# Two cross-attention layers: in the first layer, even entries hold their image tokens before their text tokens, and one product group makes the image values of both mixed tiles

## The chip, the cores and the metric

The kernel runs on one core of a Trainium2 chip. A core has a matrix engine (TensorE, PE in the profile; its weight loads are listed apart as PEld), a vector engine (VectorE, DVE), a scalar engine (ScalarE, ACT), GpSimd (POOL) and SyncE (SP), which here only issues transfers. Products land in PSUM banks; all else lies in SBUF, 128 partitions wide, or in DRAM. Transfers are carried by the core's sixteen DMA engines. The metric is the device time of one execution in microseconds, as the median of several runs.

## What is computed

Two attention layers follow each other, over B = 16 entries of S = 256 query rows with C = 320 channels and H = 20 heads of D = 16. Both read the same context of 256 tokens of width 512 for each entry. The change concerns the first layer alone:

```python
TEXT_LEN, SEM_SCALE = 77, 0.5
text = encoder_hidden_states[:, :TEXT_LEN]      # 77 tokens
ip = encoder_hidden_states[:, TEXT_LEN:]        # 179 tokens
q = hidden_states @ Wq
k_text, v_text = text @ Wk, text @ Wv
...
text_out = softmax(q_h @ k_text_h * scale) @ v_text_h          # by heads
...
text_probs = softmax(q @ k_text * scale)                       # all channels at once
sem = (text_probs @ text) @ ip * scale
fused = q_h @ ip_k_h * scale + SEM_SCALE * sem[:, None]        # ip_k = ip @ Wk_ip
ip_probs = softmax(fused) * spatial_mask
out = (text_out + ip_probs @ ip_v_h) @ Wout + bout + residual  # ip_v = ip @ Wv_ip
```

So every query attends to 77 text tokens and to 179 image tokens, with a softmax of its own for each kind and other weights for keys and values of each kind. The second layer is alike, with 252 text and 4 image tokens; it is not touched.

## The kernel before

**Slots.** The first layer is worked off in 80 slots: 16 entries times five groups of four heads, slot k being group k % 5 of entry k // 5. In the middle of the first layer ten slots, that is two entries or one pair, take some 75 us. Into the gaps between the attention steps of a slot the function `fill` puts steps of tasks that prepare later entries: each task has a list of times, in slots, at which its steps are due. TensorE's instructions stand in the order in which this text issues them; a scheduler orders the other engines, within the dependencies.

**The context of a pair.** Entries are prepared two at a time. `context` loads the transposed context of a pair, four blocks of 128 of the 512 input rows by 2 x 256 tokens, into tiles `ct` (tags `cta`, `ctb`), and splits it into a rounded high part and the rest, as every product is made of three (high times high, high times low, low times high). In such a tile the first entry's text comes first, then its image, then the second entry's text and image.

**Values.** `values0_` (L412) makes the values of an entry as three tiles of 128 tokens by 320 columns: tile 0 is tokens 0 to 127 with the text weights (`wv0`), tile 1 the same tokens with the image weights (`wvi0`), tile 2 tokens 128 to 255 with the image weights. Tokens 0 to 127 are mixed, 77 text and 51 image, so this mixed tile is made twice, once for each kind, and ACT's copy out of PSUM multiplies by a mask of rows that keeps text rows in the one and image rows in the other. Each tile is a group of twelve products (four blocks, three terms). The 17th column of every head in these tiles holds a mark, the mask itself, which gives the sums of the softmax; it is written once at the start (`marks`).

**Keys and stacks.** `keys0` makes the keys of a pair, text with `wk0` and image with `wki0`, and sends them to DRAM. For each slot `stacks0` (L697), called four slots ahead (`LEAD`), builds two stacks in SBUF, for four heads side by side: in the key stack (`ks`, four buffers in turn) rows 0 to 47 are the keys, rows 48 to 124 the matrix M of the entry (half the products of its 77 text tokens with its image tokens; zero for text columns), rows 125 and 126 two indicator rows, -1 for text and for image tokens. In the query stack (`qs`) stand the queries, the text probabilities (`tph`, 77 rows), and the maxima of the scores. M is made by `tokens0` (L424). A slot needs M and `tph` anew for the first four of an entry's five groups; the fifth finds them in its buffer. The text columns of rows 48 to 124 are set to zero once, at the start, and M's transfer writes the image columns alone (L710); the indicator rows too are written once for each of the four buffers (`fields`, L343). All of SP's transfers are issued by the helper `dma`, so L83 is their line in the profile, and their tiles tell them apart: M's are `ks<-M`.

**A slot's attention.** `score0` (L730) multiplies rows 0 to 124 of both stacks for two slots ahead, and DVE takes the maxima over text (L738) and image columns (L739). `maxima0` (L741) turns them with a small product (L745), ACT copies them out (L747) and sends them into the query stack's last two rows (L749, `qs<-mt`). `turned0` (L751) multiplies all 127 rows into turned scores (L761), from which the indicator rows take the maxima; ACT makes exponentials (L764) and POOL multiplies them by a correction (L767). `attend0` multiplies them with the value tiles (L794), and `settle0` divides (L805 and on).

The order of a slot k on TensorE is: maxima of slot k + 1, first half of the scores of slot k + 2, first half of the turned products of slot k, prepared steps, attention of slot k - 1, second half of the scores, second half of the turned products, then the stacks of slot k + 4 are asked for, and prepared steps again.

Of the kernel before, what the change touches and what calls it, by code (L numbers as in the profile page):

```python
# [17 lines left out]
S = 256  # L18
H = 20
# [7 lines left out]
T1 = S - NIP  # L27
DUP = S // 2 - NIP
# [21 lines left out]
def xattn2(  # L50
# [60 lines left out]
    words, slots = {"ctb": 1024, "cta": 1024, "raw": 512, "rawc": 512, "both": 2 * (S - T0), "kb": 936, "si": 256, "sp": 128, "wC": 2 * 4 * (H * D + NIP), "mt": S, "mx": 2, "tmp": (NG + 1) * 48, "kst": 4 * S, "rs": 2 * S, "P": 4 * S}, {}  # L111
# [77 lines left out]
    def in_turn(parts, wait, tag="raw", eng=nc.vector, later=False):  # L189

        ahead, parts, tags = [], list(parts), tag.split()
        for i in range(len(parts) + 1):
            if len(tags) > 1:
                new = () if i else range(len(parts))
            else:
                new = range(i + 1 if i else 0, min(i + 2, len(parts)))
            if i:
                halves(*ahead.pop(0), eng, wait)
            for j in new:
                src, hi, lo = parts[j]  # L200
                raw = buf(tags[j // 2 % len(tags)], [128, 512], bufs=2)
                shape = src.shape
                raw = raw[:, : shape[1]] if len(shape) == 2 else raw.rearrange("p (k n) -> p k n", k=shape[1])
                (queued if later else lambda inst: inst)(dma(raw, src))
                ahead.append((hi, lo, raw))
            if wait:
                yield
# [53 lines left out]

    def context(b, n, wait=0):

        tiles, parts = [], []
        for k in range(0, 4, 3 - n):
            src = cT_d[:, b * S : (b + n) * S].rearrange("(k p) t -> p k t", p=128)[:, k : k + 3 - n]
            ct = buf("cta" if n == 1 or k < 2 else "ctb", [128, 2, 512], FR, bufs=SIZES["CTA" if n == 1 or k < 2 else "CTB"], name="ct")
            split = lambda t: t.rearrange("p (k t) -> p k t", t=n * S)
            parts.append((src, split(ct[:, 0]), split(ct[:, 1])))
            tiles.append(ct)  # L270
        yield from in_turn(parts, wait, "rawc raw" if b == 2 and n == 2 else "rawc", nc.gpsimd if wait and b != 2 else nc.vector, n == 2 and b > 2)
        if n == 2:
            return lambda s, k: tiles[k][:, s].rearrange("p (b t) -> p b t", b=2)
# [12 lines left out]
    ct = [buf(t, [128, 2, 512], FR, bufs=2, name="ct") for t in ("cta", "cta", "ctb", "ctb")]  # L286
    ct0 = {0: lambda s, k, tiles=ct: tiles[k][:, s].rearrange("p (b t) -> p b t", b=2)}
# [27 lines left out]
    hsn = const_tile([128, 3, 8, 2, 16], "hsn")  # L315

    def constants():
# [3 lines left out]
        for i in range(SIZES["NR"]):  # L321
            nc.gpsimd.memset(f(ks[i]), 0.0)
# [10 lines left out]

    def fields():
# [7 lines left out]
        for i in range(SIZES["NR"]):  # L342
            dma(ks[i][XROW + T0 : KS0], ind0r.unsqueeze(1).to_broadcast([2, 4, S]))  # L343
# [16 lines left out]
    def keys0(c):  # L360
# [8 lines left out]
        for m in range(3):  # L369
            kst = buf("kst", [128, 2, 2, S], FR, bufs=SIZES["KST"])  # L370
            for w, lo, hi, a, z in ((wk0, 0, T0 + 1, 0, T0), (wki0, T0 - 1, S, T0, S)):
                kp = bank()[:, : 2 * (hi - lo)].rearrange("p (b t) -> p b t", b=2)
                prod_m(kp, w, m, lambda s, k: ct(s, k)[:, :, lo:hi], 4)
                n = 64 if m == 2 else 128
                evacuate(kst[:, 0, :, a:z], kst[:, 1, :, a:z], kp[:, :, a - lo : z - lo], m)
                if a:
                    keys_out(kd[0][c], m, kst)
                else:
                    nc.gpsimd.tensor_copy(kt[:n, m, :, :, :T0], f(kst[:n, :, :, :T0]))
                yield  # L380

    def keys_first():

        ct = ct0[0]
# [27 lines left out]
    def values0_(b):  # L412
        ct, i = ct0[b // 2], b % 2
        V = vr[(b + 2) % 3]
        for t, (w,), lo, sc in ((0, wv0, 0, tmask[:, 0:1]), (1, wvi0, 0, tmask[:, 1:2]), (2, wvi0, 128, 1.0)):
            vp = bank()[:, :320]
            prod(vp, lambda s, k: ct(s, k)[:, i, lo : lo + 128], lambda s, k: w(s, k), 4)
            nc.scalar.activation(
                vcols(V, V0W)[:, t, :, 0:16], vp.rearrange("p (h d) -> p h d", d=D), AF.Copy, scale=sc
# [4 lines left out]
    def tokens0(b):  # L424

        ct, i = ct0[b // 2], b % 2
        M = buf("M", [T0, 2, S], FR, bufs=SIZES["M"])
        nc.gpsimd.memset(f(M[:, :, :T0]), 0.0)
        gp = bank()
        lo = 64  # L430
        prod(gp[:T0, : S - lo], lambda s, k: ct(s, k)[:, i, :T0], lambda s, k: ct(s, k)[:, i, lo:S], 4)
        src = gp[:T0, T0 - lo : S - lo]
        nc.scalar.activation(M[:, 0, T0:], src, AF.Copy, scale=0.5)
        nc.vector.scalar_tensor_tensor(M[:, 1, T0:], src, 0.5, f(M[:, 0, T0:]), op0=ALU.mult, op1=ALU.subtract)
# [211 lines left out]
    def semantic0(b):  # L646
# [40 lines left out]
        for t in range(2):  # L687
            mm(rp[:, t], mh[:, 0, t * 128 : (t + 1) * 128], tph[:, 1], start=True, stop=False)
            mm(rp[:, t], mh[:, 1, t * 128 : (t + 1) * 128], tph[:, 0], start=False, stop=True)
# [7 lines left out]
    def stacks0(k, parts="KQTM"):  # L697
        b, g = divmod(k, NG)
        Q, K = QK[k] = qs[k % SIZES["NR"]], ks[k % SIZES["NR"]]
        for part in parts:  # L700
# [4 lines left out]
            elif g < SIZES["NR"]:  # L705
# [3 lines left out]
                else:  # L709
                    dma(K[XROW : XROW + T0, :, T0:], mh[:, 0:1, T0:].to_broadcast([T0, 4, S - T0]))  # L710
# [19 lines left out]
    def score0(k, t):  # L730
# [7 lines left out]
        nc.vector.tensor_reduce(mn[:, t, :, 0], sp[:, :, :T0], axis=AX.X, op=ALU.max)  # L738
        anchor(nc.vector.tensor_reduce(mn[:, t, :, 1], sp[:, :, T0:], axis=AX.X, op=ALU.max))  # L739
# [50 lines left out]
    def values0(k, pv, v, vt):  # L790
        t, o = ((0, 0), (0, S), (1, S))[vt]
        for s in range(4):
# [335 lines left out]
    for c in range(B // 2):  # L1128
# [7 lines left out]
        task(("v0", 2 * c), shifted(n, -7, -5.4, -5), lambda b=2 * c: values0_(b), *k)  # L1136
# [261 lines left out]
```

## Time and profile before

| | us |
|---|---|
| median of three runs | 1509.85 |
| lowest and highest run | 1503.91, 1513.44 |
| profiled execution, its time | 1522.64 |
| profiled execution, its span | 1520.8 |

| engine | busy us of the span |
|---|---|
| PE | 1436.6 |
| POOL | 1215.1 |
| DVE | 1178.0 |
| ACT | 884.4 |

The profile is of one execution. Its span runs from the first to the last instruction; the time beside it has what lies around the span too. Rows of instructions give the line, the engine, the operation, the tiles as out<-in, the shapes as partitions by elements, how many there were, their busy time together in us and the mean of one in ns, then the idle time of the engine just before them and what ended it. Matmuls overlap each other, so the time from one group's start to the next group's start says what a group costs, not the duration of its instructions. Rows of a timeline give start and duration in us. Rows of a stretch give its length, then each engine's busy time with the number of instructions, then the clock that was granted to TensorE as a share of the full one, the mean busy share of the sixteen DMA engines, and what they moved in GB/s. SPq and ACTq are the queues on which SP and ACT issue transfers.

### The profile page before, as it was taken

The page shows a single profiled execution, that of the slowest core. Times are in us where ns is not written, and L with a number is a line of the kernel's source. Part 1 is how long each engine was busy: PE and PEld are TensorE (multiplying, and loading weights), DVE is VectorE, ACT ScalarE, POOL GpSimd, SP SyncE. Part 2 cuts the span into 40 slices and gives each one's busy share as a digit, 9 for nine tenths or more (in the row PEclk, how much of TensorE's full clock was granted, in tenths as well). Part 3 has the DMA queues.
Part 4 walks back from the last instruction along what each step waited for, and adds up shares of the span by engine and source line. Part 5 has one row for each costly group of instructions (what it writes and reads, how often), then busy time and mean ns, then how long its engine had stood idle before and what let it go on. Part 6 is the DMA issues. An engine that isn't in the chain of part 4 may idle for free.

```text
span 1520.8 us, 36025 instructions
## 1 busy us (share of the span) xinstructions
PE 1436.6 (94%) x12726; PEld 1160.9 (76%) x12726; DVE 1178.0 (77%) x2595; ACT 884.4 (58%) x1973; POOL 1215.1 (80%) x1302
## 2 busy tenths in 40 slices
PE   8689999999999989788999999999999999999996
PEld 7678878887888778566777777777777777777764
DVE  5467777777777787867878888888888887788885
ACT  5346555655565555445665666566656666666561
POOL 4359787978888977887688789877988798879785
PEclk9899999999999999899999999999999999999997
DMA  7757766767676766665534444444444344434311
GB/s 237 208 165 216 203 192 197 214 204 209 183 213 210 210 194 172 186 198 156 147 104 120 125 124 118 130 122 114 121 134 124 107 125 131 125 108 113 103 33 37
DMA packets 228815, 233.04 MB, mean 153 GB/s; under 512 B 38410, under 2 KB 198508, under 8 KB 228620
## 3 DMA queue, kind: packets, MB, share of 16 engines
q1 hardware_dynamic: 226428, 229.44, 52.7%
q8 instruction: 102, 1.67, 0.5%
q10 hardware_dynamic: 2208, 1.30, 0.3%
q14 instruction: 77, 0.63, 0.1%
HBM read 118.04 MB, written 77.10 MB: 128 GB/s over the span
## 4 chain that ended last, share of the span: by engine, by line
PE 75%; DVE 7%; DMA 6%; issue 4%; POOL 3%; ACT 3%; SPq 1%; ACTq 0%; DVEq 0%; POOLq 0%
PE X L932 15%; PE X L238 14%; PE P L794 6%; PE X L603 5%; PE P L944 5%; PE S L737 5%; PE P L954 4%; PE T L761 4%; PE T L884 3%; PE S L890 3%; PE X L606 2%; PE X L248 2%; PE X L572 2%; DMA qs<-mt 1%; PE X L1057 1%
## 5 line engine op out<-in xcount | busy, mean ns | idle before, releaser
L767 POOL TENSOR_TENSOR P<-P,rs 128x512 f32<-128x512 f32 x320 | 415.1, 1321 | 102.5 <-ACT P L764 101.5
L923 POOL TENSOR_TENSOR wt<-P,ctb 128x512 f32<-128x512 f32 x320 | 410.3, 1307 | 78.4 <-ACT ctb L922 78.3
L932 PE MATMUL X<-ctb,gm 128*128 128x512 f32 x1120 | 305.6, 402 | 5.9 <-DVE wt L933 5.8
L764 ACT ACTIVATE P<-T 128x512 f32<-128x512 f32 x320 | 175.9, 593 | 158.6 <-PE T L761 100.0
L933 DVE TENSOR_TENSOR wt<-X,wt 128x512 f32<-128x512 f32 x320 | 216.3, 681 | 42.9 <-PE X L932 37.5
L932 PEld LDWEIGHTS X<-ctb,gm 128*128 128x128 f32 x1120 | 195.7, 189 | 39.1 <-DVE wt L933 8.5
L904 ACT ACTIVATE P<-T 128x512 f32<-128x512 f32 x320 | 173.1, 593 | 77.3 <-PE T L884 75.0
L922 ACT ACTIVATE ctb<-P 128x512 fp32r<-128x512 f32 x320 | 186.9, 627 | 38.8 <-PE X L932 35.4
L892 DVE TENSOR_REDUCE mn<-S 128x4 fp32r<-128x1008 f32 x160 | 191.4, 1196 | 0.0
L739 DVE TENSOR_REDUCE mn<-S 128x4 fp32r<-128x716 f32 x160 | 142.4, 890 | 0.0
L794 PE MATMUL P<-P,vr 128*32 128x256 f32 x1920 | 129.5, 402 | 2.2 <-DVE tmp L811 1.9
L737 PE MATMUL S<-ks,qs 125*128 125x256 f32 x640 | 117.5, 307 | 6.0 <-DVE mn L739 1.7
L737 PEld LDWEIGHTS S<-ks,qs 125*128 125x128 f32 x640 | 88.2, 194 | 41.9 <-issue 21.9
L761 PE MATMUL T<-qs,ks 127*128 127x256 f32 x640 | 108.6, 291 | 4.9 <-DMA qs<-mt 3.2
L1020 POOL TENSOR_TENSOR r<-u,rs 128x40 f32<-128x40 f32 (+2 forms) x17 | 108.7, 6395 | 3.6 <-DVE u L1017 3.6
L805 DVE STREAM_TRANSPOSE nt<-P 128x512 f32<-128x512 f32 x80 | 57.0, 713 | 56.8 <-PE P L794 56.3
L761 PEld LDWEIGHTS T<-qs,ks 127*128 127x128 f32 x640 | 91.5, 196 | 7.6 <-ACT P L764 2.1
L738 DVE TENSOR_REDUCE mn<-S 128x4 fp32r<-128x308 f32 x160 | 74.6, 466 | 28.2 <-PE S L737 27.8
L794 PEld LDWEIGHTS P<-P,vr 128*32 128x32 f32 x1920 | 57.7, 114 | 45.6 <-issue 9.5
L944 PE MATMUL P<-P,v1t 128*32 128x256 f32 x1280 | 86.3, 388 | 0.0
L954 PE MATMUL P<-wt,zone 128*32 128x256 f32 x1280 | 84.8, 379 | 0.3 <-DVE wt L933 0.3
L603 PE MATMUL X<-ho,wF 128*128 128x256 f32 x512 | 75.3, 289 | 9.2 <-ACT mt L747 4.7
(279 smaller groups left out, 2987.6 us busy)
## 6 DMA issues: line engine op xcount, KB each, us to landing
qd<-q SPq DMA_DIRECT2D x96, 256.0 KB
qs<-tph SPq DMA_DIRECT2D x64, 308.0 KB
rawc<-in_cT_dram SPq DMA_DIRECT2D x60, 256.0 KB
qs<-qd SPq DMA_DIRECT2D x80, 192.0 KB
ks<-kd SPq DMA_DIRECT2D x80, 192.0 KB
ks<-kd SPq DMA_DIRECT2D x160, 96.0 KB
qs<-qd SPq DMA_DIRECT2D x160, 96.0 KB
kd<-kst SPq DMA_DIRECT2D x57, 256.0 KB
```

What stands on the lines that cost most here:

```text
L238: last = mm(out, lhs(a, k), rhs(b, k), start=i == 0, stop=i == len(terms) - 1)
L737: mm(sp[:, h], Q[: XROW + T0, h, t * 128 : (t + 1) * 128], K[: XROW + T0, h], start=True, stop=True)
L761: mm(st[p][:, j], K[:KS0, 2 * p + j, t * 128 : (t + 1) * 128], Q[:KS0, 2 * p + j], start=True, stop=True)
L764: exp = anchor(nc.scalar.activation(pt, st[p], AF.Exp, scale=SCALE))
L767: anchor(nc.gpsimd.tensor_mul(pt, pt, rs[:, t : t + 1].to_broadcast([128, 2, S])))
L794: mm(pv[32 * s : 32 * s + 32, o : o + S], v[:, vt, h : h + 32], P[k, s // 2][:, t, s % 2], start=vt < 2, stop=vt != 1,)
L892: anchor(nc.vector.tensor_reduce(maxes[k + 2][:, t], sp[:, :, :T1], axis=AX.X, op=ALU.max))
L904: anchor(nc.scalar.activation(P[k, u][:, t], st[u], AF.Exp, scale=SCALE))
L922: nc.scalar.activation(R[k, u][:, t], P[k, u][:, t], AF.Copy, scale=0.5)
L923: anchor(nc.gpsimd.tensor_sub(W[k, u][:, t], P[k, u][:, t], f(R[k, u][:, t])))
L932: mm(yp, gm[:, gb], R[k, u][:, kt], start=i == 0, stop=i == len(blocks[n]) - 1)
L933: nc.vector.tensor_mul(W[k, u][:, n], yp, W[k, u][:, n])
```

## The change

In pairs 1 to 7 (entries 2 to 15) the context tile gets another order: image tokens of the first entry (179), a gap of 26 columns that stays zero or is masked, image tokens of the second entry, text of the first, text of the second, zeros. `pair` names two runs of such a tile at once. Columns 128 to 255 of it then hold the last 51 image tokens of the first entry, the gap, and the first 51 image tokens of the second. For the first entry of the pair (`turned_round`), tokens stand image first: its tile of tokens 0 to 127 is all image, its mixed tile is tokens 128 to 255, with 51 image and 77 text rows. The second entry keeps text first. One group of twelve products with the image weights on columns 128 to 255 gives the image values of both mixed tiles, which ACT copies out twice, with a mask for each. Six groups of value products for a pair become five.

With it go these:

- Each context load of a pair becomes two transfers (image runs and text runs), and the split works on 538 instead of 512 columns.
- The text keys' products are 154 instead of 156 columns wide.
- As the order of tokens now differs between entries, the text columns of M and the indicator rows differ too. The tile M gets two more rows, which hold the indicators, and its transfer writes all 256 columns of 79 rows of the key stack, where it wrote 179 columns of 77 rows. The zeroing of the four key stacks and the four transfers of indicator rows at the start go; two small transfers fill the two M tiles at the start, and two more turn one of them round at entry 2.
- The marks of the value tiles are written by POOL for each entry from 2 on, as the masks differ by entry, two small copies each.
- Times of the value steps move: for even entries from -7, -5.4, -5 to -7, -5.4, -4.4, for odd ones from -4, -3.8, -3.4 to -3.4, -2.4.

In the built programs, TensorE has 84 products 128x320 with the image weights fewer, and SP has 64 transfers `ks<-M` of 79x4x256 where it had 64 of 77x4x179.

```diff
+LI = S - T0
+IB, TA = 205, 384
+TB, TE = TA + T0, TA + 2 * T0
+CW = TB + 128
...
+    def pair(a, start, stride, n):
+
+        (row, rows), (step, _) = a.ap
+        return type(a)(a.tensor, a.offset + start * step, [[row, rows], [stride * step, 2], [step, n]])
+
+    def turned_round(b):
+
+        return b > 1 and b % 2 == 0
+
+    def text_image(b):
+
+        return (slice(LI, S), slice(0, LI)) if turned_round(b) else (slice(0, T0), slice(T0, S))
...
+                row = cT_d[k * 128 : (k + 1) * 128, b * S : (b + 2) * S].rearrange("p (b t) -> p b t", b=2)
+                to = lambda raw: (pair(raw, 0, IB, LI), raw[:, TA:TE].rearrange("p (b t) -> p b t", b=2))
+                src = [(lambda raw: to(raw)[0], row[:, :, T0:]), (lambda raw: to(raw)[1], row[:, :, :T0])]
+                parts.append((src, ct[:, 0, :TE], ct[:, 1, :TE]))
...
-        for i in range(SIZES["NR"]):
-            nc.gpsimd.memset(f(ks[i]), 0.0)
+        for t in slack:
+            nc.gpsimd.memset(f(t), 0.0)
...
-        for i in range(SIZES["NR"]):
-            dma(ks[i][XROW + T0 : KS0], ind0r.unsqueeze(1).to_broadcast([2, 4, S]))
+        for i in range(2):
+            fused.append(buf("M", [T0 + 2, 2, S], FR, bufs=SIZES["M"]))
+            dma(fused[i][T0:, 0], ind0r)
...
     def values0_(b):
         ct, i = ct0[b // 2], b % 2
         V = vr[(b + 2) % 3]
-        for t, (w,), lo, sc in ((0, wv0, 0, tmask[:, 0:1]), (1, wvi0, 0, tmask[:, 1:2]), (2, wvi0, 128, 1.0)):
+
+        def product(w, at, *to):
             vp = bank()[:, :320]
-            prod(vp, lambda s, k: ct(s, k)[:, i, lo : lo + 128], lambda s, k: w(s, k), 4)
-            nc.scalar.activation(
-                vcols(V, V0W)[:, t, :, 0:16], vp.rearrange("p (h d) -> p h d", d=D), AF.Copy, scale=sc
+            prod(vp, lambda s, k: ct(s, k)[:, at : at + 128], lambda s, k: w[0](s, k), 4)
+            for v, t, sc in to:
+                nc.scalar.activation(
+                    vcols(v, V0W)[:, t, :, 0:16], vp.rearrange("p (h d) -> p h d", d=D), AF.Copy, scale=sc
+                )
...
+        if turned_round(b):
+            product(
+                wvi0,
+                128,
+                (V, 1, masks[1]),
+                (vr[(b + 3) % 3], 1, tmask[:, 1:2]),
             )
             yield
         return V
...
-        M = buf("M", [T0, 2, S], FR, bufs=SIZES["M"])
-        nc.gpsimd.memset(f(M[:, :, :T0]), 0.0)
+        text, image = text_image(b)
+        M = buf("M", [T0 + 2, 2, S], FR, bufs=SIZES["M"])
+        if b == 2:
+            for to, at in ((text, slice(0, T0)), (image, slice(T0, S))):
+                dma(M[T0:, 0, to], fused[1][T0:, 0, at])
+        nc.gpsimd.memset(f(M[:T0, :, text]), 0.0)
...
-                    dma(K[XROW : XROW + T0, :, T0:], mh[:, 0:1, T0:].to_broadcast([T0, 4, S - T0]))
+                    dma(K[XROW : XROW + T0 + 2], mh[:, 0:1].to_broadcast([T0 + 2, 4, S]))
...
     def values0(k, pv, v, vt):
         t, o = ((0, 0), (0, S), (1, S))[vt]
+        if turned_round(k // NG):
+            t = 1 - t
```

108 lines of the change are left out of this document (73 added, 35 removed).

## The prediction

> **What bounds the kernel now.** I read the page first: its span, the busy time of the engines and the chain of waits that ended last.
>
> ```profile
> span 1520.8 us, 36025 instructions
> PE 1436.6 (94%) x12726; PEld 1160.9 (76%) x12726; DVE 1178.0 (77%) x2595; ACT 884.4 (58%) x1973; POOL 1215.1 (80%) x1302
> PE 75%; DVE 7%; DMA 6%; issue 4%; POOL 3%; ACT 3%; SPq 1%; ACTq 0%; DVEq 0%; POOLq 0%
> ```
>
> The reader is to see that three quarters of the last chain is TensorE. Then I asked for busy times by stretches, because the change touches the first layer alone.
>
> ```profile
> core 0: us, PE busy (x) PEld busy (x) DVE busy (x) ACT busy (x) POOL busy (x), PEclk, DMA share, GB/s
> 250.00:300.00 50.00, 49.75 (x475) 42.45 (x474) 36.96 (x90) 30.48 (x73) 44.39 (x43) 1.00 0.68 201
> 30.00:670.00 640.00, 591.94 (x5349) 503.43 (x5348) 471.46 (x1066) 345.21 (x816) 503.49 (x504) 0.96 0.69 198
> ```
>
> In the steady part TensorE is busy 49.75 of 50 us at full clock, POOL 44.39, and the sixteen DMA engines are on average busy 0.68 of the time. The second row is the stretch in which the first layer sends its M tiles into the key stacks, from the first such transfer to the last; it is, but for the first transfer of the 64, the stretch that this prediction is about. TensorE sets its length; the transfers have room, but as an average over sixteen engines.
>
> **The product groups that go.** The timeline of TensorE shows one group of twelve 128x320 products with the image weights wD, from its first product to the next line's:
>
> ```profile
> 346.88 1.05 PE L238 MATMUL X<-wD,cta 128*128 128x320 f32 x6
> 347.76 1.04 PE L238 MATMUL X<-wD,ctb 128*128 128x320 f32 x6
> 348.74 1.50 PE L794 MATMUL P<-P,vr 128*32 128x256 f32 x24
> ```
>
> That is 348.74 - 346.88 = 1.86 us. Seven pairs of entries lose one group each: 7 x 1.86 = 13.0 us of TensorE. While TensorE sets the pace all of it would be gained. The text keys' products go from 156 to 154 columns, which I count as nothing. The value steps move later by 0.6 to 1 slot and are still made slots before their entry starts; nothing late comes of that.
>
> **What the other engines get.**
>
> ```profile
> L163 ACT CAST cta<-rawc 128x512 fp32r<-128x512 f32 x46 | 26.5, 629 | 4.6 <-DMA rawc<-in_cT_dram 4.6
> L166 POOL TENSOR_TENSOR cta<-rawc,cta 128x512 fp32r<-128x512 f32 x42 | 55.2, 1316 | 4.7 <-ACT cta L163 4.7
> L322 POOL MEMSET ks<- 128x1024 f32 x4 | 3.7, 954 | 0.0
> L332 POOL COPY vr<-tmask 128x20 f32<-128x20 f32 x6 | 1.4, 301 | 3.5 <-DMA tmask<-in_tmask_dram 3.5
> ```
>
> POOL writes 28 more columns of marks, 28 x 0.30 = 8.4 us; its 24 subtractions are 538 instead of 512 wide, 24 x 1.316 x 26/512 = 1.6 us; four memsets of 1024 columns go (3.8 us) and four of 154 come (0.6 us by their width). Net 6.8 us, over a stretch in which POOL idles 640 - 503 = 137 us: nothing, and at most 6.8 us if that idle time lay elsewhere than the new work. ACT's 28 casts grow by 0.03 us each, 0.9 us, with ACT busy 345 of 640. Each of the 28 context loads becomes two transfers of shorter runs and the same bytes; SP has that many more to issue, and nothing waits for them that does not already wait.
>
> The alignment of VectorE and POOL can also shift. At one place in twenty slots the trace has this:
>
> ```profile
> 214.12 3.62 DVE L283 SCALAR_TENSOR_TENSOR hq<-hq,tmask,xq 128x256 fp32r<-128x256 f32 x1
> 217.94 2.17 PE L238 MATMUL X<-cta,wB 128*128 128x360 f32 x6 [2.50 <-DVE sp L663]
> ```
>
> An operation stretched to 3.62 us holds TensorE for 2.50 us. Such places may come or go with any reordering, some 2.5 us each either way; I take none.
>
> **The transfer of the M tile.** Here the change adds what I think decides. These are the transfers and their sizes (KB of 1024 bytes):
>
> ```profile
> qs<-tph SPq DMA_DIRECT2D x64, 308.0 KB
> ks<-M SPq DMA_DIRECT2D x64, 215.4 KB
> ```
>
> The second row is 77 partitions by 4 by 179 columns. In the changed program it is 79 partitions by 4 by 256, since the two indicator rows now travel with it and the text columns too: 79 x 4 x 1024 = 323.6 thousand bytes (the 308.0 KB above are 315.4 thousand, the 215.4 KB 220.5), again 64 times. The bytes alone would be harmless. The number of rows isn't. Issues of SP and three short stretches in which one transfer alone was moving:
>
> ```profile
> 117.26 0.38 SPq L83 DMA_DIRECT2D xq<-in_xT_dram  x1
> ...
> 330.08 0.86 SPq L83 DMA_DIRECT2D qs<-tph  x1
> 330.98 0.84 SPq L83 DMA_DIRECT2D ks<-M  x1
> ...
> 336.41 0.86 SPq L83 DMA_DIRECT2D ks<-M  x1
> ```
>
> ```profile
> 331.60:332.80 1.20, 1.20 (x13) 1.20 (x11) 1.20 (x6) 0.50 (x3) 1.20 (x2) 1.00 0.69 201
> 337.92:338.60 0.68, 0.68 (x7) 0.68 (x6) 0.00 (x0) 0.05 (x1) 0.68 (x1) 1.00 0.69 180
> 118.50:119.70 1.20, 1.20 (x15) 0.84 (x8) 0.70 (x2) 0.00 (x0) 1.20 (x2) 1.00 0.84 266
> ```
>
> The first is the 77-row tph transfer issued at 330.08, the second the 77-row M transfer of 336.41, the third a 128-row load. Both 77-row transfers, of different sizes, hold the share at 0.69, which is 11/16; the 128-row load goes past it to 0.84. So 77 rows run on eleven engines, seven rows each. Sixteen engines with at most five rows each would have been quicker, and weren't used: the rows are dealt out in equal whole shares. 79 is prime. Dealt out the same way, all 79 rows go to one engine.
>
> [...]
>
> What one engine carries in a microsecond: 201/(0.69 x 16) = 18.2 GB/s in the first stretch, 266/(0.84 x 16) = 19.8 in the third. No row shows an engine working alone, so I take the fastest: 323.6/19.8 = 16.3 us for a transfer; by the slower one 17.8 us. That it is the same engine each time no row tells; I take it so, and keep the other case as a rival. Then 64 x 16.3 = 1043 us of that engine.
>
> The engine has its other work too. Over the 640 us a mean engine is busy 0.69 x 640 = 442 us. Of that the two 77-row transfers take 315.4/201 = 1.57 and 220.5/180 = 1.22 us on eleven of sixteen engines, a mean of 2.79 x 64 x 11/16 = 123 us; one of the eleven keeps the tph part, 1.57 x 64 = 100 us. So 442 - 123 + 100 = 419 us. Spread over twice the time the engines get in each other's way less: at 19.8 GB/s instead of the stretch's 198/(0.69 x 16) = 17.9 it is 379 us.
>
> Sum: 1043 + 379 = 1422 us of one engine, where the whole stretch now takes 640. Is it in the way? These rows show the slack:
>
> ```profile
> 345.87 0.69 PE L737 MATMUL S<-ks,qs 125*128 125x256 f32 x4
> ...
> 350.74 0.65 PE L761 MATMUL T<-qs,ks 127*128 127x256 f32 x4
> ```
>
> The M transfer issued at 336.41 belongs to the stack four slots ahead, whose first score products come two slots later, at 345.87: 9.5 us after the issue, against 16.3 us of moving. TensorE then waits in L737 for the landing; behind it in TensorE's order stand the turned products, the attention products and every projection, ACT waits for the turned products, POOL for ACT, and SP's next stack transfers for the products that read the buffer. On the engine itself the next K, Q and tph transfers and the x loads stand behind the M rows. The next M but one is issued some 5.5 us after L737 starts (350.74 + 0.65), before the one in between is through, so the engine is rarely without work, and its sum is the stretch: 1422 us for 640, 782 us more. The 13.0 us of products are then hidden in TensorE's waiting and count nothing, like POOL's 6.8.
>
> The profiled execution took 1522.6 us, 1.8 more than its span, and the median of the runs shown is 1509.85, 12.8 less. In the profile's terms 1522.6 + 782 = 2305; against the median 1510 + 782, about 2290 us.
>
> Bounds. If an engine alone were a fifth faster than the fastest row (my estimate, no row shows it), 64 x 13.1 + 379 = 1215, so 2085. At 17.8 us and 419 us, 1558, so 2428; after each entry's fourth M transfer there is a slot without one, in which the engine may idle 5.5 us, 16 x 5.5 = 88, so 2516.
>
> [...]
>
> **The rivals.** *The rows are spread after all.* If a count like 79 is dealt out with a remainder, or padded, from four engines on a transfer takes 16.3/4 = 4.1 us, fits the 9.5 us, and the products' 13.0 us are gained: 1510 - 13 = 1497, 0.8% less. For it: nothing, no such count is in the trace; against it: eleven engines for 77.
>
> *One engine for each transfer, but another each time.* Then only the latency counts. Two slots now last from the row below to 345.87, 14.6 us, 7.3 each:
>
> ```profile
> 331.31 0.69 PE L737 MATMUL S<-ks,qs 125*128 125x256 f32 x4
> ```
>
> Moving starts 1.5 us after the issue (336.41 to 337.92) and takes 16.3 us; the products up to the next issue but one take 5.5: 23.3 us for two slots, 11.7 each, 4.4 more. 64 x 4.4 = 282 us: 1792. The 0.69 doesn't tell which eleven engines work.
>
> *ACT's small transfers are held up too.* Each slot's maxima reach the query stack in four of these:
>
> ```profile
> qs<-mt ACTq DMA_DIRECT2D x312, 2.0 KB
> ```
>
> They have two rows and another queue. If they too had to wait until the M rows are through, nothing of a slot would overlap with its M: 1.5 + 16.3 + 5.5 + 379/80 = 28.0 us for 64 slots and some 8 for the other 16, 1920 us, 1280 more: 2790. Against it: a queue of their own and 2 KB.
>
> **How the numbers follow.** I give the forecast 0.84, the spread rows 0.05, the changing engine 0.05, the held-up small transfers 0.06. The time is the forecast's, 2290. The range is that of its bounds, 2090 to 2520, and leaves out the rivals and the edge of the forecast, about 0.2. A measurement of this kernel can tell about 1% from no change. Slower by over 1% are all cases but the spread rows: 0.95; of those 0.05, 0.03 lie within 1% and 0.02 beyond it, if stalls like the one at 217.94 go as well.
>
> **What would show it.** In the changed kernel's profile: the stretch from the first to the last M transfer at about 1400 us, the rest as before; TensorE's idle time before L737's successor (the score products) released by the M transfer, some 10 us a slot in four slots of five; the DMA share falling to about 0.3 while M rows move alone, with stretches near 1/16 = 0.06 at 18 to 20 GB/s; L238's wD products fewer by 84; TensorE's clock often below 1. I am wrong if stretches with an M transfer alone show a share well above 0.06, or if the score products don't wait for it.

## The result, and the profile after

The changed kernel takes 2301.6 us in the median (2300.0 to 2304.2, 4 runs) where the kernel before takes 1511.6 us on the same chip (1503.9 to 1517.6, 4 runs): 1.523 times as long, 95% interval 1.516 to 1.531. Its profiled execution took 2301.9 us, 779.3 more than the profiled execution before. The forecast was 2290 us, with 2305 for the profiled execution. One execution of a version below, of 1549.0 us, was in a slower state of the chip and is left out of that version's figures.

The page of the changed kernel: span, busy time, TensorE's share and clock and the DMA share in 40 slices of 57.5 us, and the chain that ended last.

```profile
span 2300.0 us, 35908 instructions
PE 1584.2 (69%) x12642; PEld 1265.5 (55%) x12642; DVE 1220.4 (53%) x2597; ACT 885.1 (38%) x1973; POOL 1211.2 (53%) x1334
...
PE   7265555545545555554654544799999999999997
...
PEclk8577777667777776776777776899999999999999
DMA  5433323333333333323333332544443434444331
...
DMA 40%; PE 38%; SPq 10%; DVE 5%; POOL 2%; issue 2%; ACT 1%; ACTq 0%; DVEq 0%; POOLq 0%
DMA ks<-M 15%; DMA qs<-tph 13%; PE X L1010 10%; SPq L87 10%; PE X L249 6%; PE P L1022 3%; DMA qs<-qd 3%; PE X L678 3%; PE P L1032 3%; DMA ks<-kd 2%; PE T L962 2%; PE S L968 2%; DVE hq L313 2%; PE S L812 2%; DMA qd<-q 1%
```

The first 25 slices are the first layer, and only they have changed: TensorE's share falls to about one half, its granted clock mostly to 0.6 to 0.7, and the DMA engines, which are what everyone waits for, are on average *less* busy than before (0.33 in the first row below, where it was 0.69). The chain was three quarters TensorE; now 40% of it is transfers, with the M tile at their head, and 10% is SP's own issuing. Here the low DMA share beside a chain of transfers means that few of the sixteen engines are in use; the stretches show how few.

```profile
core 0: us, PE busy (x) PEld busy (x) DVE busy (x) ACT busy (x) POOL busy (x), PEclk, DMA share, GB/s
30.00:1440.00 1410.00, 735.52 (x5264) 606.07 (x5263) 514.89 (x1074) 345.46 (x815) 501.26 (x530) 0.71 0.33 96
1486.00:2300.00 814.00, 786.44 (x6919) 606.36 (x6917) 659.32 (x1400) 497.76 (x1057) 661.04 (x722) 0.99 0.40 113
605.00:612.00 7.00, 6.18 (x45) 4.92 (x44) 3.44 (x9) 1.50 (x5) 5.05 (x6) 0.77 0.07 22
```

The stretch with the M transfers takes 1410 us instead of 640, and within it the engines do the work that they did before in 640 us (POOL 501 us against 503). The second row begins where the last attention product of the first layer ends. In the kernel before, the part behind that product is

```profile
708.80:1520.80 812.00, 786.01 (x6918) 607.20 (x6917) 659.52 (x1401) 497.38 (x1057) 660.89 (x722) 0.99 0.41 113
```

so 777 of the 779.2 us between the spans lie ahead of it, in the first layer. The last row of the three lies inside one M transfer: the share is 0.07, about one sixteenth, and 22 GB/s are moved. Counted from the trace's packet records between 400 and 1200 us, exactly one packet is in flight about half of the time and none about 5% of it.

SP's queue around that transfer (start, duration, instruction):

```profile
602.57 0.74 SPq L87 DMA_DIRECT2D ks<-M  x1
603.36 10.42 SPq L87 DMA_DIRECT2D qs<-tph  x1
613.84 0.86 SPq L87 DMA_DIRECT2D ks<-kd  x1
614.74 0.96 SPq L87 DMA_DIRECT2D qs<-qd  x1
...
622.89 0.75 SPq L87 DMA_DIRECT2D ks<-M  x1
```

M itself is issued in 0.74 us, but the tph transfer behind it keeps SP for 10.42 us, where before it took 0.86. The trace does not say why; that SP could not put it in while M's rows fill the one engine is the author's guess. So K and Q rows are not even issued until some two thirds of M's 316 packets have gone, and the next M follows 20.3 us later. The waits of the changed kernel (total, times, longest) show what that does further on:

```profile
PE S L812 <- DMA qs<-qd: 167.6, 22, 13.0
PE S L812 <- DMA qs<-mt: 54.4, 6, 10.1
PE S L812 <- DMA ks<-M: 9.6, 1, 9.6
```

```profile
ACT P L840 <- DMA qs<-tph: 89.8, 8, 15.3
ACT P L840 <- DMA qs<-mt: 86.1, 8, 14.5
ACT P L840 <- DMA ks<-M: 83.6, 6, 14.8
```

TensorE's score products (now L812) wait longest for the Q rows, which SP issues last, and only once for M itself.

### The profile page after: what moved, and what is told of

It reads as the page before. It is cut to its first block, busy times and chain, and to the rows that moved or that the text cites. A ratio compares the mean times of both kernels' runs of the same rounds, so it can differ in the third digit from the quotient of the medians.

```text
span 2300.0 us, 35908 instructions
## 1 busy us (share of the span) xinstructions
PE 1584.2 (69%) x12642; PEld 1265.5 (55%) x12642; DVE 1220.4 (53%) x2597; ACT 885.1 (38%) x1973; POOL 1211.2 (53%) x1334
## 4 chain that ended last, share of the span: by engine, by line
DMA 40%; PE 38%; SPq 10%; DVE 5%; POOL 2%; issue 2%; ACT 1%; ACTq 0%; DVEq 0%; POOLq 0%
DMA ks<-M 15%; DMA qs<-tph 13%; PE X L1010 10%; SPq L87 10%; PE X L249 6%; PE P L1022 3%; DMA qs<-qd 3%; PE X L678 3%; PE P L1032 3%; DMA ks<-kd 2%; PE T L962 2%; PE S L968 2%; DVE hq L313 2%; PE S L812 2%; DMA qd<-q 1%
## 5 line engine op out<-in xcount | busy, mean ns | idle before, releaser
L843 POOL TENSOR_TENSOR P<-P,rs 128x512 f32<-128x512 f32 x320 | 410.0, 1301 | 588.8 <-ACT P L840 588.4
L812 PE MATMUL S<-ks,qs 125*128 125x256 f32 x640 | 151.4, 372 | 326.1 <-DMA qs<-qd 167.6
L812 PEld LDWEIGHTS S<-ks,qs 125*128 125x128 f32 x640 | 115.6, 251 | 373.9 <-issue 133.3
L837 PE MATMUL T<-qs,ks 127*128 127x256 f32 x640 | 145.4, 355 | 45.3 <-ACT P L840 38.9
L872 PE MATMUL P<-P,vr 128*32 128x256 f32 x1920 | 154.2, 464 | 2.2 <-DVE tmp L889 1.5
L837 PEld LDWEIGHTS T<-qs,ks 127*128 127x128 f32 x640 | 121.2, 250 | 55.9 <-ACT P L840 41.3
L821 PE MATMUL X<-ident_r,mn 128*8 128x128 f32 x160 | 28.4, 249 | 175.0 <-DVE M L509 60.1
L821 PEld LDWEIGHTS X<-ident_r,mn 128*8 128x8 f32 x160 | 14.3, 93 | 183.9 <-DVE M L509 61.7
L170 DVE TENSOR_TENSOR kst<-X,kst 128x252 fp32r<-128x252 f32 (+2 forms) x64 | 26.6, 417 | 153.6 <-ACT kst L167 140.2
L872 PEld LDWEIGHTS P<-P,vr 128*32 128x32 f32 x1920 | 63.2, 130 | 61.8 <-issue 34.0
```

The costliest lines, as they stand in the source:

```text
L812: mm(sp[:, h], Q[: XROW + T0, h, t * 128 : (t + 1) * 128], K[: XROW + T0, h], start=True, stop=True)
L837: mm(st[p][:, j], K[:KS0, 2 * p + j, t * 128 : (t + 1) * 128], Q[:KS0, 2 * p + j], start=True, stop=True)
L843: anchor(nc.gpsimd.tensor_mul(pt, pt, rs[:, t : t + 1].to_broadcast([128, 2, S])))
L872: mm(pv[32 * s : 32 * s + 32, o : o + S], v[:, vt, h : h + 32], P[k, s // 2][:, t, s % 2], start=vt < 2, stop=vt != 1,)
```

## Experiments

Three explanations were to be told apart: the *row count* (79 rows go to one engine), the *bytes* (47% more of them, whole rows of the key stack), and the *order* (the entries turned round, with its added loads, marks and moved steps). Each run was timed beside the kernel before on the same chip, where that took 1511 to 1515 us in the median; the ratios are to that, with their 95% intervals.

**One row more.** The tile and the transfer get an 80th row, which nothing reads (a copy of an indicator row).

```diff
-        M = buf("M", [T0 + 2, 2, S], FR, bufs=SIZES["M"])
+        M = buf("M", [T0 + 3, 2, S], FR, bufs=SIZES["M"])
...
-                    dma(K[XROW : XROW + T0 + 2], mh[:, 0:1].to_broadcast([T0 + 2, 4, S]))
+                    dma(K[XROW : XROW + T0 + 3], mh[:, 0:1].to_broadcast([T0 + 3, 4, S]))
```

> The changed kernel with one unused row more in the M tile and its transfer: 80 rows of 1 KB x 4 instead of 79 (327.7 thousand bytes instead of 323.6). Theory 'row count' (79 rows can only be dealt out to one engine, 80 go to sixteen with five rows each): the M transfer takes 20.5 KB per engine, about 1.1 us, the wait in front of the score products goes, the time is 1497 to 1510 us (the 13.0 us of products may come out in full or in part), DMA share from 30 us to the last M transfer about 0.7. Rival 'bytes' (what costs is the larger transfer, or that it writes whole rows of the key stack): stays near 2300. Rival 'order' (the new order of the even entries, its added casts, memsets and loads): stays near 2300.

Measured: 1533.4 us, 1.0128 times before (1.0093 to 1.0163). One more row takes 768 us off. The stretch in this kernel's profile:

```profile
30.00:670.00 640.00, 579.43 (x5157) 487.37 (x5157) 466.99 (x1050) 340.14 (x803) 498.89 (x519) 0.94 0.73 205
```

The share is 0.73 and TensorE busy 579 of 640 us again. A stretch in which one 80-row M transfer moves, issued at 257.32, has nearly all sixteen engines at work:

```profile
259.00:259.70 0.70, 0.70 (x8) 0.70 (x8) 0.70 (x4) 0.15 (x1) 0.70 (x2) 1.00 0.99 257
```

Row count it is; but the time is 20 us *above* the kernel before, where up to 13 below were expected. That second finding needed experiments of its own, further down.

**The same 79 rows as 77 and 2.**

```diff
-                    dma(K[XROW : XROW + T0 + 2], mh[:, 0:1].to_broadcast([T0 + 2, 4, S]))
+                    for a, z in ((0, 77), (77, 79)):
+                        dma(K[XROW + a : XROW + z], mh[a:z, 0:1].to_broadcast([z - a, 4, S]))
```

> The changed kernel with the M tile sent as two transfers, 77 rows and the two indicator rows, same bytes to the same places. 'Row count': eleven and two engines, 11 x 7 rows in about 1.6 us, so 1497 to 1515 us. SP issues 64 transfers more, 0.4 to 0.9 us each, for which it has room. 'Bytes' and 'order': near 2300.

Measured: 1561.4 us, 1.0316 (1.0281 to 1.0350). The large cost goes here too, with the same bytes to the same places. The time is above the range expected of the row count, 1497 to 1515: eleven engines carry the 77 rows, by the share of 0.69 in the kernel before, and the next run shows that this costs something (1.0127).

**The kernel before with the bytes alone, and with the rows alone.** First the M transfer of the kernel before with all 256 columns of its 77 rows; then that kernel with the changed kernel's transfer, 79 rows by 256 columns (the tile holds the indicator rows for it), and no other part of the change.

```diff
-                    dma(K[XROW : XROW + T0, :, T0:], mh[:, 0:1, T0:].to_broadcast([T0, 4, S - T0]))
+                    dma(K[XROW : XROW + T0], mh[:, 0:1].to_broadcast([T0, 4, S]))
```

> The kernel before, with one difference: the M transfer carries all 256 columns of its 77 rows instead of the last 179 (315.4 thousand bytes instead of 220.5), still 77 rows. 'Row count': eleven engines as before, 0.5 us more a transfer, hidden: 1505 to 1515 us, same as before. 'Bytes': most of the 790 us, so 2200 to 2300. 'Order': same as before.

```diff
-                    dma(K[XROW : XROW + T0, :, T0:], mh[:, 0:1, T0:].to_broadcast([T0, 4, S - T0]))
+                    dma(K[XROW : XROW + T0 + 2], mh[:, 0:1].to_broadcast([T0 + 2, 4, S]))
```

> The kernel before, with the M tile of 79 rows and its transfer of 79 rows x 256 columns as in the changed kernel, and nothing else of the change: no other order of entries, no fewer products. 'Row count': 64 transfers of about 16 us on one engine beside some 380 us of other work there, 2270 to 2330 us. 'Bytes': likewise near 2300. 'Order': 1505 to 1520 us, as before.

Measured: 1533.6 us, 1.0127 (1.0094 to 1.0159), for the bytes; 2305.1 us, 1.524 (1.518 to 1.530), for the rows. The first-layer stretch of the second is like that of the changed kernel:

```profile
30.00:1440.00 1410.00, 742.41 (x5352) 611.06 (x5350) 509.51 (x1072) 343.84 (x816) 496.56 (x505) 0.72 0.33 95
```

So the 79-row transfer makes the whole of the 790 us by itself, and the turned order isn't needed for it. The 20 us of the 77 longer rows were not expected.

**How the time grows with the work of the one engine.** The kernel before with 79 rows but only the 179 image columns; and the changed kernel with the 79 rows sent as 74 (twice 37) and 5.

```diff
-                    dma(K[XROW : XROW + T0, :, T0:], mh[:, 0:1, T0:].to_broadcast([T0, 4, S - T0]))
+                    dma(K[XROW : XROW + T0 + 2, :, T0:], mh[:, 0:1, T0:].to_broadcast([T0 + 2, 4, S - T0]))
```

> The kernel before with the M transfer of 79 rows, but only the 179 image columns as before (226.3 thousand bytes instead of 323.6), nothing else changed. Theory 'sum of the engine': 226.3/19.8 = 11.4 us a transfer, 64 x 11.4 + 379 = 1109 us for the stretch instead of 640: about 1980 us (2160 if a packet of 716 bytes costs as much as one of 1 KB). Theory 'latency past the slack' (only what a transfer takes beyond the 9.5 us between its issue and its use costs, the rest of the engine's work being carried in gaps): 1.5 + 11.4 - 9.5 = 3.4 us a transfer, 64 x 3.4 = 218 us, about 1730 us.

```diff
-                    dma(K[XROW : XROW + T0 + 2], mh[:, 0:1].to_broadcast([T0 + 2, 4, S]))
+                    for a, z in ((0, 74), (74, 79)):
+                        dma(K[XROW + a : XROW + z], mh[a:z, 0:1].to_broadcast([z - a, 4, S]))
```

> The changed kernel with the M tile sent as 74 rows (2 x 37, so two engines) and 5 rows (five engines). One transfer then takes 37 x 4 x 1024 bytes at 19.8 GB/s = 7.7 us, within the 9.5 us from issue to use. 'Latency past the slack': as with eighty rows, about 1530 us. 'Sum of the engine': the busier engine has 64 x (7.7 + 0.2) + 379 = 885 us of work for a stretch of 640: 245 us more, about 1760 to 1780 us.

Measured: 2085.2 us and 1856.8 us. In both the time is more than 300 us above what latency past the slack would cost. The engine's sum is the right kind of price, and some 80 to 105 us short at both points. (For the first, 2160 us had been named too, if a packet of 716 bytes cost as much as one of 1 KB: in the packet records of the kernel before it takes 35 ns in the median against 46, so it costs less than that, but more than in proportion to its bytes.) The tph transfer goes out once for each M, so the row of its 64 issues (shortest, median and longest issue in ns; first and last start) measures the stretch. Before:

```profile
L83 SPq DMA_DIRECT2D qs<-tph x64: 837/867/939, 32.5 to 663.0; - x64
```

The changed kernel:

```profile
L87 SPq DMA_DIRECT2D qs<-tph x64: 882/9930/10657, 41.5 to 1424.2; - x64
```

79 rows of 179 columns:

```profile
L83 SPq DMA_DIRECT2D qs<-tph x64: 877/896/8425, 38.8 to 1214.6; - x64
```

74 and 5 rows:

```profile
L87 SPq DMA_DIRECT2D qs<-tph x64: 846/879/1982, 33.5 to 990.2; - x64
```

From first to last that is 631, 1383, 1176 and 957 us: it falls with the bytes on the busiest engine (324, 226 and 156 thousand a slot for the last three; the 156 is an estimate, 38 x 4 x 1024 for 37 rows of the 74 and one of the five, as no view shows these transfers moving alone). The median of the tph issue, 9.93 us in the changed kernel and under 1 us in the other two, does not mean that SP is no longer held there. It is held at whatever stands right behind M, with 179 columns at the K rows:

```profile
605.17 0.69 SPq L83 DMA_DIRECT2D ks<-M  x1
605.91 7.91 SPq L83 DMA_DIRECT2D ks<-kd  x1
```

In the changed kernel 51 tph issues and 8 of K rows take more than 2 us, 591 us together; with 179 columns it is 53 of K rows, 6 of Q rows and 2 of tph, 537 us. So no run here has the full engine without the held queue. That the engine's bytes set the pace is read from the stretches, which grow by 207 us from 179 columns to the changed kernel, where the holding grows by 54.

**Is it always the same engine?** The 79 rows as 31, 31 and 17, three primes.

```diff
-                    dma(K[XROW : XROW + T0 + 2], mh[:, 0:1].to_broadcast([T0 + 2, 4, S]))
+                    for a, z in ((0, 31), (31, 62), (62, 79)):
+                        dma(K[XROW + a : XROW + z], mh[a:z, 0:1].to_broadcast([z - a, 4, S]))
```

> The changed kernel with the M tile's 79 rows sent as three transfers of 31, 31 and 17 rows, all prime. Theory 'always the same engine' (each prime count goes to one engine, and it is the same one each time): the engine's sum stays, 79 rows x 4 packets a slot, so 2290 to 2320 us, and the DMA share while only M rows move stays near 1/16 = 0.06. Rival 'another engine for the next transfer': the three move beside one another, 31 x 4 x 1024 bytes at 19.8 GB/s = 6.4 us a slot, and an engine has on the mean a third of the 64 x 16.3 us: 348 + 379 = 727 us for a stretch of 640, about 1600 to 1650 us, DMA share up to 3/16 = 0.19.

Measured: 2206.5 us, 1.458 (1.449 to 1.467). A stretch with such transfers under way, and SP's issues of the three (shortest, median and longest issue in ns; first and last start):

```profile
632.00:640.00 8.00, 5.85 (x56) 4.76 (x54) 4.60 (x11) 2.52 (x6) 5.42 (x5) 0.90 0.08 26
L87 SPq DMA_DIRECT2D ks<-M x3: 757/1672/5477, 630.3 to 632.8; - x3
```

The first two are issued by 632.8 us, and the third's issue is held from there to 638.3. So two transfers are under way for most of the stretch, then three, and the share is 0.08 of sixteen engines, not 2/16 = 0.13 or more: they share one engine. In time, the rival with another engine each time falls by some 550 us. The 95 us under the changed kernel go with fewer moments in which nothing moves: counted from the packet records as above, under 3% instead of 5%; that this is the cause was not tried. The tph issues give this run's stretch:

```profile
L87 SPq DMA_DIRECT2D qs<-tph x64: 886/913/4375, 37.4 to 1325.1; - x64
```

That is 1288 us, with the same M rows on the same engine that has 1383 us in the changed kernel.

**Where the 20 us at eighty rows come from.** The kernel before with eighty M rows, once with 256 and once with 179 columns.

```diff
-                    dma(K[XROW : XROW + T0, :, T0:], mh[:, 0:1, T0:].to_broadcast([T0, 4, S - T0]))
+                    dma(K[XROW : XROW + T0 + 3], mh[:, 0:1].to_broadcast([T0 + 3, 4, S]))
```

> The kernel before with the M tile and transfer of 80 rows x 256 columns: sixteen engines with 20.5 KB each, where the 77 rows of 179 columns put 20.0 KB on each of eleven. Nothing of the new order. If the 20 us that the 77 rows of 256 columns cost come from the eleven engines' longer transfers (28.7 KB each), they go: 1505 to 1518 us, and the 20 us of the changed kernel with eighty rows are then the order's own. If they come from the bytes as such, it stays at 1525 to 1540 us, and the order is worth nothing either way.

> The kernel before with the M transfer of 80 rows x 179 columns: 14.3 KB on each of sixteen engines instead of 20.0 KB on each of eleven, 4% more bytes. If M's time on its engines matters at all near 1510 us, it is a little faster than before, 1495 to 1508 us; if there is slack, 1505 to 1518 us.

Measured: 1510.9 us, 0.9987 (0.9962 to 1.0012), and 1513.6 us, 0.9986 (0.9963 to 1.0010). Neither differs from before. So the 256 columns cost nothing when sixteen engines share them and 1.3% when eleven do. In the waits, 77 rows of 256 columns have

```profile
PE S L737 <- DMA qs<-qd: 5.8, 9, 1.4
```

and with eighty rows that wait is not among those listed; but these 5.8 us are not 20, and with eighty rows there are 4.9 us of waits for M instead, so the waits don't show where the 20 us of the eleven engines arise. The 20 us of the changed kernel with eighty rows are then the own cost of the new order with all that goes with it. Together the two make 40 of the 48 us that the 77 and 2 rows cost; the other 8 were not looked into. Three parts of the order were tried. First the seven product groups were put back, the order staying:

```diff
-        if turned_round(b):
-            product(
-                wvi0,
-                128,
-                (V, 1, masks[1]),
-                (vr[(b + 3) % 3], 1, tmask[:, 1:2]),
-            )
+        if b > 1:
+            product(wvi0, 128, (V, 1, masks[1]))
             yield
...
-        task(("v0", 2 * c + 1), shifted(n, -3.4, -2.4), lambda b=2 * c + 1: values0_(b), *k)
+        task(("v0", 2 * c + 1), shifted(n, -4, -3.4, -2.4) if c else shifted(n, -3.4, -2.4), lambda b=2 * c + 1: values0_(b), *k)
```

> The changed kernel with eighty M rows, and the seven groups of twelve image products back: each entry of a turned pair makes the image values of its mixed tile itself, the order of the entries stays. Theory 'TensorE sets the pace' (the prediction's: whatever TensorE no longer does is gained while no transfer holds it): 7 x 1.86 = 13.0 us more than the eighty rows' 1533, so 1541 to 1551 us. Rival 'the other engines set it as much' (POOL, VectorE, ACT and the transfers are so near their own limits there that the products fall into idle time): 1528 to 1538 us, the same.

Measured: 1521.0 us, 1.0033 (1.0009 to 1.0057). Both theories miss: with 13 us more of TensorE's work the kernel is 12 us *faster*, and the two intervals, 1.0009 to 1.0057 and 1.0093 to 1.0163, lie apart. The stretch from 110 to 700 us, with the shared products:

```profile
110.00:700.00 590.00, 545.83 (x4984) 459.07 (x4981) 449.40 (x1009) 325.06 (x761) 493.09 (x517) 0.96 0.74 208
```

and with each entry's own:

```profile
110.00:700.00 590.00, 558.88 (x5182) 474.96 (x5181) 462.18 (x1036) 336.35 (x779) 504.96 (x527) 0.98 0.74 210
```

The second kernel finishes more instructions on every engine in the same 590 us, TensorE idles 31 us instead of 44, at a clock of 0.98 instead of 0.96. Part of that gap is of the executions that were profiled: the first is the slowest of its six, 1540.5 us, 7 above its median, the second is at its median. The step with the products also stands at other due times and in another entry in the two; whether the fewer products or the moved step makes the idle time was not tried.

Second, in the kernel before with eighty rows, the 28 context loads were cut in two, as in the change:

```diff
-                (queued if later else lambda inst: inst)(dma(raw, src))
+                cut = [slice(None)] if not (later or tag == "rawc raw") else [slice(T0, S), slice(0, T0)]
+                for z in cut:
+                    halved = lambda ap: ap.rearrange("p o (b t) -> p (o b) t", b=2)[:, :, z] if len(cut) > 1 else ap
+                    (queued if later else lambda inst: inst)(dma(halved(raw), halved(src)))
```

> The kernel before with eighty M rows (1511 us), and 28 context loads cut in two, image and text columns of both entries apart, to the same places: packets of 716 and 308 bytes instead of 2 KB, as in the changed kernel; nothing of the new order. If the split loads are what the changed kernel with eighty rows pays (SP's 28 issues more, four packets for one), most of its 22 us: 1525 to 1540 us. If nothing waits for them, as the prediction says: 1506 to 1516 us.

Measured: 1532.6 us, 1.0091 (1.0061 to 1.0121), against 0.9987 for the same kernel with whole loads: about 16 us. In its profile TensorE's wait for sp grows; whole loads first, cut loads second:

```profile
PE X L238 <- DVE sp L667: 2.4, 2, 1.5
```

```profile
PE X L241 <- DVE sp L670: 13.0, 5, 3.2
```

Over all of TensorE's waits that the view lists, those for VectorE grow from 36.8 us with whole loads to 53.7 with cut ones, and those for transfers go from 14.9 to 12.1. One of the places, on VectorE, on POOL and on TensorE (start, duration, line, operation):

```profile
143.91 3.38 DVE L286 SCALAR_TENSOR_TENSOR hq<-hq,tmask,xq 128x256 fp32r<-128x256 f32 x1 [0.56 <-ACT hq L284]
147.66 0.22 DVE L670 TENSOR_TENSOR sp<-sp,X 128x77 f32<-128x77 f32 x1
```

```profile
141.60 3.77 POOL L774 TENSOR_TENSOR P<-P,rs 128x512 f32<-128x512 f32 x3
145.32 0.46 POOL L819 TENSOR_TENSOR hsn<-tmp 128x128 f32<-128x128 f32 x1
145.73 1.27 POOL L285 TENSOR_TENSOR hq<-xq,hq 128x512 fp32r<-128x512 f32 x1
```

```profile
147.93 2.17 PE L241 MATMUL X<-cta,wB 128*128 128x360 f32 x6 [3.17 <-DVE sp L670]
```

VectorE's L286 takes 0.6 us in the median. Here it starts while POOL works without a gap and ends at 147.29, just after POOL's run ends at 147.00; then sp follows late, and TensorE has idled 3.17 us. At two more places of this profile it takes 3.63 us from 223.99 and 3.93 from 302.90, and there too it ends 0.28 and 0.29 us after a run of POOL (221.94 to 227.34 and 299.88 to 306.54). That POOL's run is what holds it is the author's reading of these places; no row names a cause. So most of what the cut loads cost shows as waits for VectorE, and not as waits for transfers. That the cut loads move VectorE's instruction to where POOL has a longer run is argued from this one profile: the kernel before's own profile has such places too (the prediction shows one of 3.62 us, which ends 0.29 us after POOL's run from 210.79 to 217.45), with whole loads. And in the changed kernel with eighty rows TensorE's listed waits have none for this sp, so what its 20 us consist of stays open.

Third, the changed kernel with eighty rows, its marks written by VectorE instead of POOL:

```diff
-                nc.gpsimd.tensor_copy(vcols(V, V0W)[:, t, :, 16], sc.to_broadcast([128, H]))
+                nc.vector.tensor_copy(vcols(V, V0W)[:, t, :, 16], sc.to_broadcast([128, H]))
```

> The changed kernel with eighty M rows, its 28 columns of marks written by VectorE instead of POOL (28 x 0.30 = 8.4 us of POOL less). If POOL is the second bound that the order's additions press on: 8 to 10 us less than the eighty rows' 1533, so 1521 to 1527 us. If POOL has the room that the prediction gave it: 1529 to 1538 us.

Measured: 1527.0 us (1520.6 to 1538.1), 1.0074 (1.0043 to 1.0105). It lies at the upper edge of the first expectation, but the interval meets that of the eighty rows, 1.0093 to 1.0163: not settled.

## Why the prediction was right

**The mechanism.** "79 is prime. Dealt out the same way, all 79 rows go to one engine" was the step that carried everything, and it holds: eighty rows take the 768 us away, 77 and 2 take most of them away, and the transfer alone puts all of them into the kernel before. The inference from a share of 0.69 = 11/16 was enough to see it. The counts whose share was read fit equal whole shares of the rows: 0.69 for 77 rows, 0.07 for 79, 0.99 for 80. That it is the same engine each time, which the prediction took without a row for it, is shown by the primes: with two and then three such transfers under way the share was 0.08.

**The transfer's price** was mis-sized, and the error was nearly cancelled by another. 16.3 us came from 19.8 GB/s; one engine alone moved 22 GB/s (window 605 to 612), so 323.6/22 = 14.7 us and 64 x 14.7 = 941 us, 102 less than forecast. The idle time of that engine, which the forecast put at nothing and its bound at 88 us, is at least the share in which no packet moves, about 5% of 1410, so some 70 to 80 us. 941 + 379 + 80 = 1400 us for 1410 measured and 1422 forecast. The 379 us of the engine's other work was not measured by itself; the run with the primes, where 941 us of M rows and all the rest fit into 1288 us and a slot of some 20, leaves at most about 370 for it. That an engine carries more where fewer are at work, on which the 379 us lean, fits two rows: 22 GB/s alone, 257/(0.99 x 16) = 16.2 with all sixteen; what slows them no row tells. So the mechanism was right, and that the forecast of 2290 us came within 12 us of the measurement is luck in part: a transfer priced some 10% too high made up for idle time that was left out.

**The rest of the kernel** was forecast as unchanged, and it is: 814 us against 812 behind the first layer's last attention product, at a clock of 0.99 in both.

**Who waits** was right only in part. The score products were to be released by the M transfer, some 10 us in four slots of five. They mostly wait for the Q rows (167.6 us in 22 waits), which SP issues after the held tph transfer, and next for the maxima's small transfers (54.4 us); M itself ended one wait, of 9.6 us, and three waits of their weight loads, of 37.3 us together. The prediction had said that it would be wrong "if the score products don't wait for it", and by this sign this step of it failed for the most part. It named the transfers that stand behind M on the engine; that SP itself would be held at issue was missing. The sum of the engine's work did not need it.

**The products' 13.0 us.** "The 13.0 us of products are then hidden in TensorE's waiting" holds for the changed kernel: with 79 rows it takes 2302 us, the kernel before with 79 rows 2305. The condition stated earlier, "While TensorE sets the pace all of it would be gained", was not borne out. The profile of the changed kernel shows the products gone, 2 x 150 where there were 2 x 192:

```profile
L249 PE MATMUL X<-wD,cta 128*128 128x320 f32 x150 | 27.1, 317 | 0.3 <-ACT vr L462 0.3
L249 PE MATMUL X<-wD,ctb 128*128 128x320 f32 x150 | 26.2, 310 | 0.0
```

But with eighty rows the time without them is 12 us above the time with them (the moved step is in that difference too). So the rival "rows spread after all" at 1497 us would have been wrong too, by about 36 us. "The bytes alone would be harmless" is right for sixteen engines and 20 us wrong for eleven. That "nothing waits for them that does not already wait", of the cut context loads, misses about 16 us in the kernel before with eighty rows, most of them in waits for VectorE; the prediction knew of VectorE's alignment with POOL and took none for it. None of this shows behind 790 us.

**The other rivals.** Another engine each time, 1792 us: refuted by the three primes, and by the 2302 us measured. ACT's small transfers held up, 2790 us: they are at times (86.1 us of ACT's waits in 8, up to 14.5 us, where before the longest was 2.8), not in each slot.

## What to carry over

When rows are added to a tile that a DMA sends, look at the factors of the new row count before anything else: 77 rows went to eleven engines (share 0.69), 79 to one (0.07), 80 to sixteen (0.99), and in the kernel before eighty rows cost nothing (0.9987). A falling DMA share (0.69 to 0.33) beside a chain of transfers was the sign of it here, and the price was at least the sum of that engine's packets over the loop, not the latency past the slack. And a busy share of 94% on TensorE didn't make its products worth their duration here (with 13 us of them back, and a step moved, the version with eighty rows took 1521 us instead of 1533): put them back in the version without the large fault and measure.

## What was not expected of the hardware

With M on a single engine, the transfer issued right behind it held the issuing queue. For the tph transfer that stands there in the changed kernel it is 9.93 us in the median against 0.87 for the same instruction before; with 179 columns it is the K rows' transfer, 7.91 us at 605.91. With eighty rows, on sixteen engines, the longest of the three kinds (tph, K rows, Q rows) took 1.7 us.

The M transfer on eleven engines, grown by 95 thousand bytes, cost 1.3% (1.0127), while the one on sixteen engines, grown by 99 thousand (80 x 4 x 77 columns of 4 bytes), cost nothing measurable (0.9987 against 0.9986).

TensorE's granted clock was lower in the stretch in which TensorE idles more: 0.71 where it is busy 736 of 1410 us, against 0.96 where it is busy 592 of 640 in the kernel before. There each product takes longer too, the score products 372 ns in the mean of the changed kernel:

```profile
L812 PE MATMUL S<-ks,qs 125*128 125x256 f32 x640 | 151.4, 372 | 326.1 <-DMA qs<-qd 167.6
```

and 307 ns in the kernel before, where TensorE is rarely idle:

```profile
L737 PE MATMUL S<-ks,qs 125*128 125x256 f32 x640 | 117.5, 307 | 6.0 <-DVE mn L739 1.7 <-DMA ks<-M 1.6 <-DMA ks<-kd 1.3
```

No version here beat the kernel before. The cheapest form of the change, with eighty rows and without the shared products, is 0.3% slower (0.1 to 0.6%).
